# A two-layer graph convolution on one core: the short group of spans moved from the end of a layer to its start, and node numbers kept in PSUM

## The chip, the cores and the metric

The kernel runs on one core of a Trainium2 chip, in one launch. The metric is the device time of an execution in microseconds. A profile was taken of one execution; its span is the time from the first to the last instruction of the program. In the profile's rows PE is TensorE (matrix products), PEld its weight loads, DVE is VectorE, ACT is ScalarE, POOL is GpSimd, and SP is SyncE. PSUM is the memory that TensorE writes its products to; SBUF is the main on-chip memory.

## What is computed

`x` has 6250 nodes with 512 features; `src` and `dst` name 100,000 edges, sorted by `dst`. All in float32:

```python
h = relu(layernorm(x))
norm = -dinv[src] * dinv[dst]                 # dinv = 1/sqrt(number of edges out of a node), 0 where none
def cheb(h, W0, W1, b):
    tx1 = segment_sum(h[src] * norm[:, None], dst)   # a sum over the edges into each node
    return h @ W0 + tx1 @ W1 + b
g = cheb(h, W1_0, W1_1, b1)
g = leaky(layernorm(g) * gamma + beta, 0.01)
out = x + cheb(g, W2_0, W2_1, b2)
```

Each of the two layers therefore needs 100,000 rows of 2 KB fetched by index and summed by destination, and two 512 x 512 products for each node.

## The kernel before

**Units of the work.** The nodes are cut into 49 blocks of 128 rows (block 48 has 106). The edges are cut into 782 chunks of 128. A chunk is fetched by one indirect DMA on GpSimd's queue (L382, `gather_to`), which brings 128 rows of 512 numbers into one of 57 buffers of the tile `places` (`zr`, used in a ring). Rows come from a table in DRAM, `tab[0]` for layer 0 and `tab[1]` for layer 1, already scaled with `dinv`; only the first 60 chunks are fetched from `x` itself and brought to scale afterwards (`look_up`, `find`).

**Units, spans and groups.** A unit is a stretch of 3 chunks (`STEP`). It sums the edges into at most 32 (`Q`) consecutive nodes, starting with the node after the last one of the chunk ahead of it. It reads a span of 4 chunks, since its last node's edges may run on into the next unit's first chunk. There are 261 units (`NU`). Four units make a group (`NQ`), because four times 32 nodes fill the 128 partitions of a PSUM tile; that gives 66 groups (`NS`). In the kernel before, group g holds units 4g to 4g+3, and the last group, 65, is left with unit 260 alone.

**One group, `sums(g)` (L461).** VectorE adds 1 to 32 to the first node number of each unit (`node`, L465) and compares these with the destinations of the span's edges (`sel`, L474): a 0/1 matrix. `first`, `iota_r`, `node`, `dlx` and `sel` all lie in SBUF. TensorE multiplies `sel` with the gathered chunks (L480), 16 products for a whole group, each in two passes, each unit on a column tile of its own of 32 columns; the loop runs over the place in the span first and over the units second, so that consecutive products go to different column tiles. ScalarE copies the sums to SBUF (`agg`, L483).

**One block, `turn` and `dense`.** `turn(layer, i)` issues loads on SP's queue for a later block, transposes the block's own rows on TensorE (`own`, L451) and has ScalarE copy them (L453). Then `place` (L485) moves the sums of the groups that can hold nodes of this block to their rows: for every such group VectorE makes a 0/1 matrix `there` (L493) and TensorE runs four products (L496). `inside[i]` lists these groups; it is worked out from the mean number of nodes per group (`GN`, 96) with a slack of 32 nodes (`DRIFT`) to both sides, and `check` (L562) counts whether the edges really keep within it (if not, the slow `general_path` runs afterwards). VectorE scales the result (`aT`, L548). `dense` runs two sets of four products, for the own rows and for the sums (L458), and `finish` adds the bias (L511 in layer 0, L506 in layer 1), and normalises, activates and stores the rows for layer 1 (layer 0), or adds `x` and stores them to `out` (layer 1). Block 48's second bias is added to `x` beforehand (L542).

**What sets the order.** TensorE, GpSimd and SP run in the order of the program (`manual_schedule`, L372); the order on VectorE and ScalarE is made by the scheduler of the language. The loop is at L624: for each group it issues gathers up to 57 chunks ahead, runs `turn` for the blocks whose last group is behind, then `sums(g)`, then `dense` for these blocks. A gather waits until the last product that reads its buffer is done. After group 64 the loop finishes block 47, takes block 48's own rows through their products (`started`), and places groups 63 and 64 for it; after group 65 only that group's sums, its placing and block 48's last products are left. Layer 1 fetches rows that layer 0 stored, so its first gather waits for block 48's store of layer 0 (L527).

Of the kernel before, what the change touches and what calls it, by code (L numbers as in the profile page):

```python
# [19 lines left out]
P = 128  # L20
# [4 lines left out]
Q = 32  # L25
# [14 lines left out]
def gnn_kernel(  # L40
# [45 lines left out]
    NS = -(-NU // NQ)  # L86
    rows = [min(P, N - i * P) for i in range(NB)]
# [47 lines left out]

    edges = ctx.enter_context(ExitStack())
# [167 lines left out]
    with tc.tile_pool(name="turn", bufs=1) as wp, tc.tile_pool(  # L304
# [14 lines left out]
        first_ps = wps.tile([P, NQ * NS + 1], F32, name="first_ps")  # L319
# [3 lines left out]
        for k in range(2):  # L323
            for q in range(NQ):
                at = STEP * (q + k)
                nc.tensor.matmul(row_ps[q * Q : (q + 1) * Q, k, :], last.to_broadcast([P, Q]),
                                 dlx[:, at : at + STEP * NQ * (NS - 1) + 1 : STEP * NQ], start=True, stop=True)
# [27 lines left out]
def usual_path(tc, have):  # L355
    nc = tc.nc
    (x, out, tab, h_tab, ndinv_d, sidx, dlx, iota_r, w_sb, W2_1, W2_0, w_late, ident, eps, ones, first, node_of, minus,
     unsorted, ln, dinv, sdinv, bias1, bias2, gam, bet, unseen, N, E, D, NB, NC, NU, NS, KD, rows, places, order,
     groups, xs, sc, pick, src_lo, src_hi, p_id, dup) = (
        have[n] for n in ("x out tab h_tab ndinv_d sidx dlx iota_r w_sb W2_1 W2_0 w_late ident eps ones first node_of "  # L360
                          "minus unsorted ln dinv sdinv bias1 bias2 gam bet unseen N E D NB NC NU NS KD rows places "
# [4 lines left out]
    GN = NQ * STEP * P * N / E  # L366
    inside = [range(max(0, math.floor((i * P - DRIFT) / GN)), min(NS, math.ceil((i * P + r + DRIFT) / GN)))
              for i, r in enumerate(rows)]
    with ExitStack() as es:
# [91 lines left out]
        def sums(g):  # L461

            n = min(NQ, NU - NQ * g)
            node = pool.tile([P, NQ, Q], F32, name="node")
            nc.vector.tensor_tensor(node[:, :n, :], first[:, NQ * g : NQ * g + n, None].to_broadcast([P, n, Q]),  # L465
                                    iota_r[:, None, 1 : Q + 1].to_broadcast([P, n, Q]), op=OP.add)
            sel = pool.tile([P, NQ, SPAN, Q], F32, name="sel")
            chunk = [range(STEP * (NQ * g + q), min(STEP * (NQ * g + q) + SPAN, NC)) for q in range(n)]
            same = n if len(chunk[-1]) == SPAN else 1
            for q in range(0, n, same):  # L470
                w = len(chunk[q])
                of = dlx[:, 1 + chunk[q][0] : 2 + chunk[q][0]]
                of = bass.AP(tensor=of.tensor, offset=of.offset, ap=[of.ap[0], [STEP, same], [1, w], [0, Q]])
                nc.vector.tensor_tensor(sel[:, q : q + same, :w, :], of,  # L474
                                        node[:, q : q + same, None, :].to_broadcast([P, same, w, Q]), op=OP.is_equal)
            ps = psum.tile([P, D], F32, name="ps")
            for s in range(SPAN):
                for q in range(n):
                    if s < len(chunk[q]):
                        nc.tensor.matmul(ps[q * Q : (q + 1) * Q, :], sel[:, q, s, :], zr(chunk[q][s]), start=(s == 0),  # L480
                                         stop=(s == len(chunk[q]) - 1))
            agg[g] = pool.tile([P, D], F32, name="agg", bufs=4)
            nc.scalar.activation(agg[g][: n * Q], ps[: n * Q], AF.Copy)  # L483

        def place(i, some):  # L485
# [4 lines left out]
            for g in some:  # L490
                m = Q * min(NQ, NU - NQ * g)
                there = pool.tile([P, P], F32, name="there", bufs=3)
                nc.vector.tensor_scalar(there[:m, :r], iota_r[:m, :r], node_of[:m, g : g + 1], -(1.0 + i * P),  # L493
                                        op0=OP.subtract, op1=OP.is_equal)
                for kc in range(KD):
                    nc.tensor.matmul(placed[i][:, kc, :r], agg[g][:m, kc * P : (kc + 1) * P], there[:m, :r],  # L496
                                     start=(g == inside[i][0] and kc == 0),
                                     stop=(g == inside[i][-1] and kc == KD - 1))

        def finish(layer, i, v):  # L500
# [10 lines left out]
            nc.vector.tensor_add(v, v, bias1[:r])  # L511
# [50 lines left out]
        def check():  # L562
# [15 lines left out]
            for at, num, by, off in ((1, min(D, NC - 1), 1, 1), (1 + D, NC - 1 - D, 1, 1),  # L578
                                     (STEP, -(-(NC - SPAN) // STEP), STEP, 2)):
                if num > 0:  # L580
# [7 lines left out]
            nc.vector.scalar_tensor_tensor(of[:, :NS], iota_r[0:1, :NS], -GN, first[0:1, : NQ * NS : NQ], op0=OP.mult,  # L588
                                           op1=OP.add)
            nc.vector.tensor_mul(of[:, :NS], of[:, :NS], of[:, :NS])  # L590
            count(of[:, :NS], OP.is_gt, float(DRIFT * DRIFT))
# [26 lines left out]
        for layer in range(2):  # L618
# [5 lines left out]
            for g in range(NS):  # L624
# [3 lines left out]
                else:  # L628
                    gather_to(layer, STEP * NQ * g + R)
# [3 lines left out]
                if layer == 0:  # L633
                    look_up("hT_ps")
                    find("hT_ps")
                    assert looked >= min(RAW, STEP * NQ * (g + 1) + 1)
# [4 lines left out]
                sums(g)  # L641
# [14 lines left out]
                if g == NS - 2:  # L656
                    while inside[i].stop < NS:
# [5 lines left out]
                    products(started[i], last_hT[layer], w_late[:, 1] if layer else w_sb[1], rows[i], True)  # L663
                    place(i, inside[i][:-1])
# [323 lines left out]
```

## Time and profile before

| | |
|---|---|
| median of 3 runs | 2149.52 us (2146.58 to 2150.33) |
| the profiled execution | 2148.89 us |
| its span | 2146.7 us |
| granted TensorE clock, mean | 0.926 of full |
| POOL busy | 1520.2 us (71%) |
| gathers from the tables (L382, x1504) | 1444.5 us, 960 ns each |
| products of the sums (L480, x4168 passes) | 732.4 us busy, 280.7 us idle ahead of them |
| placing (L496, x2080 passes) | 253.8 us busy |
| DMA over the span | 527.05 MB, mean 246 GB/s |
| gathers of layer 0, first from the table and last (start) | 172.6 us, 1087.69 us |
| gathers of layer 1, first and last (start) | 1123.74 us, 2109.66 us |

The page's group lines read: line of the kernel, engine, operation, tile written, tiles read, count | busy time, mean ns of one | idle time of the engine ahead of them, and what ended it. "issue" means that the engine waited for nothing that the profile shows. In the timeline a line is: start in us, duration in us, engine, line, operation, tiles, shapes, count, and in brackets the idle time ahead with what ended it. A float32 product shows as two passes. GpSimd's spans are those of the instruction[...], not of the transfer; a transfer lands some us after its instruction began (median 4.0 us).

### The profile page before, as it was taken

How to read it: one execution, taken by the hardware profiler on the slowest of the kernel's cores; microseconds unless marked ns; L12 is line 12 of the kernel's file. 1: busy time of each engine (PE TensorE's matmuls, PEld its weight loads, DVE VectorE, ACT ScalarE, POOL GpSimd, SP SyncE). 2: the span in 40 equal slices, each digit the busy share in tenths (PEclk: the TensorE clock that was granted, in tenths of full speed). 3: DMA queues.
4: the chain of work that ended last, by engine and by line, in shares of the span. 5: the costliest groups of instructions: out<-in, count | busy, mean ns of one | idle time of the engine just before them, and what ended most of it. 6: DMA issues, size and time to landing. Idle time of an engine off the chain costs nothing.

```text
span 2146.7 us, 23527 instructions
## 1 busy us (share of the span) xinstructions
PE 1795.7 (84%) x8843; PEld 794.7 (37%) x8843; DVE 674.8 (31%) x1341; ACT 382.7 (18%) x694; POOL 1520.2 (71%) x1577
## 2 busy tenths in 40 slices
PE   5669888988879888988876888889888888889888
PEld 4534333333334333433331333334333333334333
DVE  8974323333334233333330212212212212211211
ACT  7774212111112122111110000000000000000000
POOL 5067777777777777777727777777777777777772
PEclk9779999999989999999997989999999999999989
DMA  9298888788788888788837788888878888877883
GB/s 368 82 354 264 247 254 254 242 250 255 243 286 249 253 255 250 240 255 244 254 121 229 243 251 256 255 251 245 256 243 255 243 251 257 256 248 247 245 252 117
DMA packets 198945, 527.05 MB, mean 246 GB/s; under 512 B 31864, under 2 KB 46019, under 8 KB 198822
## 3 DMA queue, kind: packets, MB, share of 16 engines
q0 software_dynamic: 125120, 410.09, 62.4%
q1 hardware_dynamic: 73702, 115.36, 15.5%
q8 instruction: 71, 1.16, 0.2%
q14 instruction: 52, 0.43, 0.1%
HBM read 474.06 MB, written 51.27 MB: 245 GB/s over the span
## 4 chain that ended last, share of the span: by engine, by line
PE 48%; DMA 29%; POOL 9%; issue 8%; DVE 5%; ACT 0%; POOLq 0%; SPq 0%; ACTq 0%; DVEq 0%
DMA places<-tab,sidx 28%; PE u_ps L458 25%; PE ps L480 15%; POOL places L382 9%; PE aT_ps L496 5%; PE hT_ps L451 1%; DVE hi L252 1%; DVE lo L252 1%; DVE places L393 0%; PE both_ps L258 0%; DMA places<-in_x_dram,sidx 0%; DVE places L394 0%; PE u_ps L422 0%; PE hT_ps L422 0%; DVE both L428 0%
## 5 line engine op out<-in xcount | busy, mean ns | idle before, releaser
L382 POOL DMA_INDIRECT places<-tab,sidx x1504 | 1444.5, 960 | 493.8 <-issue 315.8
L480 PE MATMUL ps<-places,sel 128*32 128x512 f32 x4168 | 732.4, 666 | 280.7 <-DMA places<-tab,sidx 268.1
L480 PEld LDWEIGHTS ps<-places,sel 128*32 128x32 f32 x4168 | 141.8, 117 | 781.0 <-DMA places<-tab,sidx 591.3
L474 DVE TENSOR_TENSOR sel<-dlx,node 128x512 f32<-128x512 f32 x132 | 90.9, 688 | 750.0 <-PE ps L480 750.0
L496 PE MATMUL aT_ps<-there,agg 128*128 128x128 f32 (+2 forms) x2080 | 253.8, 278 | 1.4 <-ACT agg L483 1.4
L496 PEld LDWEIGHTS aT_ps<-there,agg 128*128 128x128 f32 (+1 forms) x2080 | 246.1, 196 | 4.2 <-ACT agg L483 3.2
L483 ACT ACTIVATE agg<-ps 128x512 f32<-128x512 f32 x132 | 78.8, 597 | 918.9 <-PE ps L480 918.9
L458 PE MATMUL u_ps<-places,hT 128*128 128x512 f32 (+1 forms) x392 | 185.8, 618 | 0.7 <-ACT hT L453 0.7
L458 PE MATMUL u_ps<-w,hT 128*128 128x512 f32 (+1 forms) x392 | 181.1, 605 | 0.7 <-ACT hT L453 0.7
L458 PE MATMUL u_ps<-places,aT 128*128 128x512 f32 (+1 forms) x392 | 178.0, 597 | 0.7 <-DVE aT L548 0.7
L458 PE MATMUL u_ps<-w,aT 128*128 128x512 f32 (+1 forms) x392 | 176.3, 592 | 0.7 <-DVE aT L548 0.7
L506 DVE TENSOR_TENSOR u_ps<-u_ps,bias 128x512 f32<-128x512 f32 x48 | 33.6, 700 | 294.9 <-PE u_ps L458 294.9
L511 DVE TENSOR_TENSOR u_ps<-u_ps,bias 128x512 f32<-128x512 f32 (+1 forms) x49 | 34.3, 700 | 284.3 <-PE u_ps L458 284.3
L453 ACT ACTIVATE hT<-hT_ps 128x512 f32<-128x512 f32 (+1 forms) x98 | 58.3, 595 | 349.6 <-PE hT_ps L451 348.2
L458 PEld LDWEIGHTS u_ps<-places,hT 128*128 128x128 f32 (+1 forms) x392 | 72.3, 195 | 117.3 <-issue 116.5
L458 PEld LDWEIGHTS u_ps<-w,hT 128*128 128x128 f32 (+1 forms) x392 | 70.3, 189 | 109.0 <-issue 106.5
L458 PEld LDWEIGHTS u_ps<-places,aT 128*128 128x128 f32 (+1 forms) x392 | 74.8, 191 | 95.4 <-issue 94.6
L458 PEld LDWEIGHTS u_ps<-w,aT 128*128 128x128 f32 (+1 forms) x392 | 74.3, 190 | 94.3 <-issue 93.4
L382 POOL DMA_INDIRECT places<-in_x_dram,sidx x44 | 45.0, 1024 | 86.8 <-ACT places L396 57.7
L448 ACT ACTIVATE h<-h,ln 128x512 f32<-128x512 f32 (+1 forms) x49 | 39.7, 813 | 283.3 <-DMA h<-in_x_dram 283.3
L493 DVE TENSOR_SCALAR there<-iota_r,node_of 128x128 f32<-128x128 f32 x260 | 76.6, 295 | 38.7 <-PE aT_ps L496 38.6
L548 DVE TENSOR_TENSOR aT<-aT_ps,to 128x512 f32<-128x512 f32 (+1 forms) x98 | 67.1, 685 | 39.4 <-PE aT_ps L496 37.9
(128 smaller groups left out, 942.7 us busy)
## 6 DMA issues: line engine op xcount, KB each, us to landing
places<-tab,sidx POOLq DMA_INDIRECT x1504
h<-in_x_dram SPq DMA_DIRECT2D x48, 256.0 KB
tab<-t SPq DMA_DIRECT2D x48, 256.0 KB
h_tab<-g SPq DMA_DIRECT2D x48, 256.0 KB
h<-h_tab SPq DMA_DIRECT2D x48, 256.0 KB
xt<-in_x_dram SPq DMA_DIRECT2D x48, 256.0 KB
out_dram<-t SPq DMA_DIRECT2D x48, 256.0 KB
places<-in_x_dram SPq DMA_DIRECT2D x4, 1792.0 KB
```

What stands on the lines that cost most here:

```text
L252: nc.vector.tensor_tensor(t, s[:, g * 2 * GJ : (g + 1) * 2 * GJ].rearrange("p (j s) -> p j s", s=2)[:, :, None, :] .to_broadcast([EP, GJ, ...
L382: nc.gpsimd.indirect_dma_start(out=zr(t), out_offset=None, in_=x if layer == 0 and t < RAW else tab[layer], in_offset=bass.IndirectOffsetO ...
L448: nc.scalar.activation(h[:r], h[:r], AF.Relu, bias=ln[:r, 1, i : i + 1], scale=ln[:r, 0, i : i + 1])
L453: nc.scalar.activation(hT[:, :, :r], ps[:, :, :r], AF.Copy)
L458: nc.tensor.matmul(u_ps[:r], hT[:, kc, :r], w[:, kc, :], start=(start and kc == 0), stop=(not start and kc == KD - 1))
L474: nc.vector.tensor_tensor(sel[:, q : q + same, :w, :], of, node[:, q : q + same, None, :].to_broadcast([P, same, w, Q]), op=OP.is_equal)
L480: nc.tensor.matmul(ps[q * Q : (q + 1) * Q, :], sel[:, q, s, :], zr(chunk[q][s]), start=(s == 0), stop=(s == len(chunk[q]) - 1))
L483: nc.scalar.activation(agg[g][: n * Q], ps[: n * Q], AF.Copy)
L493: nc.vector.tensor_scalar(there[:m, :r], iota_r[:m, :r], node_of[:m, g : g + 1], -(1.0 + i * P), op0=OP.subtract, op1=OP.is_equal)
L496: nc.tensor.matmul(placed[i][:, kc, :r], agg[g][:m, kc * P : (kc + 1) * P], there[:m, :r], start=(g == inside[i][0] and kc == 0), stop=(g ...
L511: nc.vector.tensor_add(v, v, bias1[:r])
L548: nc.vector.tensor_tensor(aT[:, :, :r], placed.pop(i)[:, :, :r], to.pop(i)[:, None, :r].to_broadcast([P, KD, r]), op=OP.mult)
```

## The change

The short group moves from the end to the start of a layer: `unit[g]` is the first unit of group g, group 0 holds unit 0 alone, and groups 1 to 65 hold four units each. Every use of the fixed stride is rewritten with it: the gathers' reach, `inside`, `place`, `row_ps` (which numbers the nodes for `there`, now in two products for each where there was one) and `check`. The bound between groups 64 and 65 gets its own, smaller slack, so that group 65 counts for block 48 alone; block 47's last group is then 64.

The first node numbers stay in PSUM, in a tile `nodes_ps` of one whole bank that lives as long as the kernel; `node` is a corner of the same tile. So L465 and L474 read one operand from PSUM and one from SBUF. `first` in SBUF stays for `check`.

`sums` is split: `choose` makes `node` and `sel`, `sums` the products. For the last group, `choose` runs ahead of block 47's work, and its products are put in the order of their chunks, not of their place in the span. Block 48's bias of layer 0 is added by a product of a row of ones with one row of `bias1` on top of its own products; the addition at L511 is left out for it.

```diff
+    unit = [max(0, NU - NQ * (NS - g)) for g in range(NS + 1)]
...
+    nodes_ps = stay.enter_context(tc.tile_pool(name="nodes_ps", bufs=1, space=bass.MemoryType.PSUM)).tile(
+        [P, D], F32, name="nodes_ps")
...
-        first_ps = wps.tile([P, NQ * NS + 1], F32, name="first_ps")
+        first_ps = nodes_ps[:, : NQ * NS + 1]
...
             for q in range(NQ):
-                at = STEP * (q + k)
-                nc.tensor.matmul(row_ps[q * Q : (q + 1) * Q, k, :], last.to_broadcast([P, Q]),
-                                 dlx[:, at : at + STEP * NQ * (NS - 1) + 1 : STEP * NQ], start=True, stop=True)
+                for g, n in ((0, 1), (1, NS - 1)):
+                    at = STEP * (unit[g] + q + k)
+                    nc.tensor.matmul(row_ps[q * Q : (q + 1) * Q, k, g : g + n], last.to_broadcast([P, Q]),
+                                     dlx[:, at : at + STEP * NQ * (n - 1) + 1 : STEP * NQ], start=True, stop=True)
...
-    GN = NQ * STEP * P * N / E
-    inside = [range(max(0, math.floor((i * P - DRIFT) / GN)), min(NS, math.ceil((i * P + r + DRIFT) / GN)))
-              for i, r in enumerate(rows)]
+    UN = STEP * P * N / E
+    mean = [UN * u for u in unit[:NS]] + [N]
+    drift = [0] + [DRIFT] * (NS - 2) + [min(DRIFT, int(mean[NS - 1]) - (NB - 1) * P), 0]
...
+        some = [g for g in range(NS) if mean[g] - drift[g] < i * P + r and mean[g + 1] + drift[g + 1] > i * P]
+        inside.append(range(some[0], some[-1] + 1))
...
-        def sums(g):
-            n = min(NQ, NU - NQ * g)
-            node = pool.tile([P, NQ, Q], F32, name="node")
-            nc.vector.tensor_tensor(node[:, :n, :], first[:, NQ * g : NQ * g + n, None].to_broadcast([P, n, Q]),
+        def choose(g):
+            at, n = unit[g], unit[g + 1] - unit[g]
+            node = nodes_ps[:, D - P :].rearrange("p (q e) -> p q e", q=NQ)
+            nc.vector.tensor_tensor(node[:, :n, :], nodes_ps[:, at : at + n, None].to_broadcast([P, n, Q]),
                                     iota_r[:, None, 1 : Q + 1].to_broadcast([P, n, Q]), op=OP.add)
             sel = pool.tile([P, NQ, SPAN, Q], F32, name="sel")
...
+                    nc.vector.tensor_tensor(sel[:, q : q + k, :w, :], of,
+                                            node[:, q : q + k, None, :].to_broadcast([P, k, w, Q]), op=OP.is_equal)
+            return sel, chunk
+        def sums(g, sel, chunk):
...
-            for s in range(SPAN):
-                for q in range(n):
-                    if s < len(chunk[q]):
-                        nc.tensor.matmul(ps[q * Q : (q + 1) * Q, :], sel[:, q, s, :], zr(chunk[q][s]), start=(s == 0),
-                                         stop=(s == len(chunk[q]) - 1))
+            todo = [(s, q) for s in range(SPAN) for q in range(n) if s < len(chunk[q])]
+            if g == NS - 1:
+                todo.sort(key=lambda t: chunk[t[1]][t[0]])
+            for s, q in todo:
+                nc.tensor.matmul(ps[q * Q : (q + 1) * Q, :], sel[:, q, s, :], zr(chunk[q][s]), start=(s == 0),
+                                 stop=(s == len(chunk[q]) - 1))
...
-            nc.vector.tensor_add(v, v, bias1[:r])
+            if i < NB - 1:
+                nc.vector.tensor_add(v, v, bias1[:r])
...
-                    gather_to(layer, STEP * NQ * g + R)
+                    gather_to(layer, STEP * unit[g] + R)
...
-                sums(g)
+                sums(g, *(chosen if g == NS - 1 else choose(g)))
...
                 if g == NS - 2:
+                    chosen = choose(NS - 1)
                     while inside[i].stop < NS:
                         dense(layer, i, *turn(layer, i))
...
                     products(started[i], last_hT[layer], w_late[:, 1] if layer else w_sb[1], rows[i], True)
+                    if layer == 0:
+                        nc.tensor.matmul(started[i][: rows[i]], ones[0:1, : rows[i]], bias1[0:1, :], start=False,
+                                         stop=False)
                     place(i, inside[i][:-1])
```

## The prediction

> **What bounds the kernel now.** I read the page first, then GpSimd's waits, then the gathers' own line, then single gathers in the timeline, and last TensorE's timeline at the end of a layer.
>
> ```profile
> PE 1795.7 (84%) x8843; PEld 794.7 (37%) x8843; DVE 674.8 (31%) x1341; ACT 382.7 (18%) x694; POOL 1520.2 (71%) x1577
> PE 48%; DMA 29%; POOL 9%; issue 8%; DVE 5%; ACT 0%; POOLq 0%; SPq 0%; ACTq 0%; DVEq 0%
> L382 POOL DMA_INDIRECT places<-tab,sidx x1504 | 1444.5, 960 | 493.8 <-issue 315.8 <-DMA places<-tab,sidx 90.9 <-DMA tab<-t 35.1
> ```
>
> The busy shares and the chain point to TensorE. The group line says otherwise: 1,504 gathers on GpSimd, 960 ns each, with 493.8 us of idle time "before" them. The question is whether that idle time is waiting. GpSimd's waits, us in total, times, longest:
>
> ```profile
> POOL places L382 <- issue: 320.7, 1052, 0.3
> POOL places L382 <- DMA places<-tab,sidx: 90.9, 298, 0.3
> POOL places L382 <- PE ps L480: 30.3, 98, 0.8
> ```
>
> 1,448 waits, and but for a single one they are the same 0.30 us, whatever is named. So it is the price of issuing a gather, and GpSimd issues back to back. From the 61st gather on, an undisturbed start-to-start step is 1.253 us (mean of the 1,433 steps under 1.29 us). Layer 1 has its first gather at 1123.74 and its last at 2109.66: 985.9 us for 781 steps, of which 781 x 1.253 = 978.6 is the bare rhythm. Layer 0 from gather 61 on: 915.1 us for 721 steps, 903.5 bare. Nothing but the rate of GpSimd sets these 1,901 us; TensorE only follows. What is above the bare rhythm is 11.6 us in layer 0 and 7.3 in layer 1, in 69 long steps. One of them, GpSimd and VectorE in the timeline:
>
> ```profile
> 1191.45 0.95 POOL L382 DMA_INDIRECT places<-tab,sidx  x1 [0.30 <-issue]
> 1192.65 0.69 DVE L474 TENSOR_TENSOR sel<-dlx,node 128x512 f32<-128x512 f32 x1 [8.59 <-PE ps L480]
> 1192.70 1.46 POOL L382 DMA_INDIRECT places<-tab,sidx  x1 [0.30 <-DMA places<-tab,sidx]
> 1194.47 0.94 POOL L382 DMA_INDIRECT places<-tab,sidx  x1 [0.30 <-DMA places<-tab,sidx]
> ```
>
> The comparison `sel` began 0.05 us ahead of the gather and ended at 1193.34; the gather took 1.46 instead of 0.95. I sorted all gathers by the VectorE instruction that was running 0.125 us after the gather began. `sel` (L474): 70 gathers, 61 of them stretched, 17.7 us in all. `node` (L465): 10, 6 stretched, 0.4. `there` (L493): 20, 5 stretched, 0.2. Instructions with one operand in PSUM and one in SBUF (L506, L507, L511, L519, L521, L525, L530, L548): 179 gathers, none stretched.
>
> The rest of the span is the two turns of a layer, in which GpSimd stands: 36.05 us from the last gather of layer 0 (1087.69) to the first of layer 1, and 37.0 from the last gather (2109.66) to the end. TensorE at the first:
>
> ```profile
> 1086.39 1.07 PE L480 MATMUL ps<-places,sel 128*32 128x512 f32 x8 [1.19 <-DMA places<-tab,sidx]
> 1087.65 1.06 PE L480 MATMUL ps<-places,sel 128*32 128x512 f32 x8 [0.19 <-DMA places<-tab,sidx]
> 1089.01 2.14 PE L480 MATMUL ps<-places,sel 128*32 128x512 f32 x10 [0.29 <-DMA places<-tab,sidx]
> 1091.08 0.66 PE L451 MATMUL hT_ps<-ident,h 128*128 128x128 f32 x4
> 1091.57 2.84 PE L496 MATMUL aT_ps<-there,agg 128*128 128x128 f32 x24
> 1094.25 3.60 PE L458 MATMUL u_ps<-w,hT 128*128 128x512 f32 x8
> 1097.69 3.60 PE L458 MATMUL u_ps<-w,aT 128*128 128x512 f32 x8
> 1101.12 0.53 PE L451 MATMUL hT_ps<-ident,h 106*128 106x106 f32 x4
> 1102.32 3.68 PE L458 MATMUL u_ps<-w,hT 128*106 128x512 f32 x8 [0.68 <-ACT hT L453]
> 1105.84 1.93 PE L496 MATMUL aT_ps<-there,agg 128*128 128x106 f32 x16
> 1107.70 1.90 PE L480 MATMUL ps<-places,sel 128*32 128x512 f32 x4
> ```
>
> Group 64 waits for chunk 780, the last but one; from there TensorE has a full queue to the last span.
>
> **Node numbers in PSUM.** `sel` and `node` each lose one SBUF input. Removed: 18.9 us of long steps, less one wait of 0.5 us on TensorE and 0.5 to 0.9 for `there` and an `is_hi`, which stay: 17.7. All of it lies on the path, since GpSimd never waits in these stretches; 0.3 more comes from gathers 32 to 60. The Trainium skill, "SBUF — State Buffer", Who interferes with whom, gives the reason: a VectorE instruction with two SBUF inputs takes a port that GpSimd needs to read SBUF, and whichever comes second waits for the whole of the first. By that rule a gather would start within a `sel` 0.693/1.253 = 55% of the time and wait 0.35 on average: 132 x 0.19 = 25 us. The rows say 17.7, since `sel` must still run 0.125 us into the gather; the rows count. Cost: `sel` 0.693 becomes about 0.70, as the additions on PSUM (L506, L511: 0.700); 134 x 0.01 us on an engine 31% busy, and `sel` is made a group ahead. Bounds: nothing gained if one SBUF input is enough to hold GpSimd, 18.5 at most. I take 18.0, because of the 179 to 0.
>
> **Setup.** `row_ps` (L326) goes from 8 products to 16, half of them one column wide; its passes now come every 0.12 us on each column tile. It delays `node_of`, and behind it the loads and the table store, by 0.1 to 0.3: take 0.2. Group 0 with one unit makes less work, early, where nothing waits for it.
>
> **More groups per block.** With boundaries shifted by 24 nodes nearly every block meets 3 groups: 290 `there` for 260, and 120 more products at L496, 240 passes x 0.11 = 27 us of TensorE. It lies in TensorE's waits for gathers (L480: 268 us). If that cover went, all 27 would count.
>
> **The last group.** Units 257 to 260 form the last group, only block 48 needs it, and block 47 needs 63 and 64. Group 64 now ends with chunk 771, ten gathers earlier; block 46's products fall behind group 64, where they were ahead of it. I write the queue from the last gather's start, G. Chunk 771 was issued at 1075.16 and landed at 1079.90 (G-7.8); in layer 1 at G-8.4. Group 64 ends 1.0 later (1090.10 to 1091.08): G-6.8 and G-7.4. Then block 46's products 7.07 (2101.88 to 2108.95), block 47's transposes and 16 placing passes 2.3 (a group fewer than the 3.2 above), its products 6.87, block 48's transposes 1.2, own products 3.5, in layer 0 the bias product 0.87 (two passes of 0.43), 8 placing passes 0.93, and the last sums. These were 2 products; they are 14, 3.7 us if they run like a full group (2098.31 to 2102.05). Sum 26.5 and 25.6: the copy of the sums starts at G+19.7 and G+18.2; it started at G+21.95 (1109.64) and G+21.92. Gains 2.2 and 3.7. In layer 0 the bias addition (L511, 0.70, plus 0.03) goes from the end: 0.7. Together 6.7. That the queue is full also means that sorting by chunk buys nothing: all chunks have landed by then.
>
> The sort may cost. In chunk order two or three products in a row go to one column tile. The Trainium skill, "TensorE: Matmul & The Clock Gate", Part 3, says matmuls start and end strictly in order. Then 19 rounds of 0.43 run where 8 do: +4.7 per layer, and both gains are gone. The trace speaks against it: L282's products go twice to the lower, then twice to the upper column tile, and their first two passes start at 87.519 and 87.532, which for one tile would be 0.1 apart. Reordering over two products is shown, over seven not. With four passes queued per tile I get +1.7; between 0 and 4.7 I take 0.8 per layer, nearer to the end the trace shows. Other uncertainty: TensorE could still be 3 us behind in layer 1, where the clock fell to 0.83 in the last stretches; and block 48's last products, 5.38 us at 2134.04 against 3.68 at 1112.11, may run 1.7 faster. Tails: 6.7 - 1.6 = 5.1, from -5.7 to 8.4. DVE stays ahead: `sel` of the last group is made before block 47, and layer 1's `sel` stands behind the last sums but ends before `aT` needs VectorE (0.98 us against 1.8).
>
> **Sum.** The profiled execution: 2148.89, of which the span is 2146.7 and 2.2 lies around it. Span 2146.7 - 18.0 - 5.1 + 0.2 = 2123.8; with 2.2: 2126.0. The median of the runs shown is 0.6 above the profiled one: 2126.6, say 2127.
>
> **Rivals.**
> *The sort eats the tails* (0.20): TensorE keeps order; 4.7 per layer lost, gain of the ports alone: 2149.5 - 18 + 3 = 2134.
> *The port is held all the same* (0.07): one SBUF input suffices; tails alone: 2144.4. Against it: 179 to 0.
> *TensorE becomes the bound* (0.05), slower: the 27 us of placing passes stretch the run if TensorE falls so far behind that a gather finds its buffer unread. With 57 buffers and 12 to a group that is some 40 gathers, 50 us. Three blocks in four groups are 4 x 3.6 + 3 x 7.7 + 9 x 0.93 = 45.9 us per 60.2 us of gathers; the clock would have to be granted under 0.76 throughout (0.95 and 0.93 in the two layers). Time: 2149.5 + 27 - 5 = 2171.
> *Gains and costs cancel* (0.06): GpSimd finds another limit near the old rate, about 2148; no row shows one.
> My case keeps 0.62.
>
> Under 0.2% (4.3 us) a measurement of this kernel can't be told from no change, so the line is at 2145.2 and 2153.8. Faster: 0.62 + 0.20 and most of the held port, 0.88; same 0.07; slower 0.05. Range: best ports and best tails give 2123, less the runs' own scatter 2120; worst tails with the ports' gain 2138.
>
> **What would show it.** Right: the gathers' mean falls from 960 to about 949 ns, no step over 1.29 with `sel` beside it, last-to-last gather about 979 us in layer 1; the pause at the turn about 33 us for 36.05. Wrong: long steps that stay (port), the 28 last passes at L480 spread over 8 us (sort), waits of GpSimd on TensorE over 0.8 us (bound).

## The result and the profile after

| | before | after |
|---|---|---|
| median of the runs on the same chip | 2148.05 us (2144.5 to 2150.33, 4 runs) | 2123.31 us (2119.62 to 2124.38, 4 runs) |
| profiled execution / its span | 2148.89 / 2146.7 us | 2123.42 / 2121.6 us |
| layer 0, from the 61st gather to the last | 915.1 us | 901.6 us |
| turn: last gather of layer 0 to first of layer 1 | 36.05 us | 34.85 us |
| layer 1, first gather to last | 985.9 us | 976.6 us |
| end: last gather to the end | 37.05 us | 36.89 us |

The ratio is 0.9887, with a 95% interval of 0.987 to 0.9904. The changed kernel is 1.1% faster; 2127 was forecast. Of the 25.1 us between the two spans, 22.8 lie in the two stretches of gathers, 1.4 in the turn and the end, and 0.9 ahead of the 61st gather. The kernel before takes 2148 to 2151 us beside the runs up to e8, but 2554 and 2529 us on the two chips of e9 to e12, so no absolute time of those four is used.

The page of the changed kernel, the lines that answer to the three shown of before, and TensorE's sums:

```profile
PE 1802.3 (85%) x9101; PEld 822.6 (39%) x9101; DVE 684.9 (32%) x1375; ACT 383.2 (18%) x694; POOL 1497.5 (71%) x1577
PE 49%; DMA 27%; POOL 10%; issue 9%; DVE 4%; ACT 0%; POOLq 0%; SPq 0%; ACTq 0%
L392 POOL DMA_INDIRECT places<-tab,sidx x1504 | 1422.5, 946 | 491.8 <-issue 314.1
L499 PE MATMUL ps<-places,sel 128*32 128x512 f32 x4168 | 714.4, 665 | 243.6 <-DMA places<-tab,sidx 234.3
```

The same 1,504 gathers take 946 ns each for 960; their idle time has hardly moved (491.8 for 493.8). TensorE has 258 more instructions and 7 us more of work, and waits for gathers 234 us. GpSimd's waits, us in total, times, longest:

```profile
POOL places L392 <- issue: 318.6, 1045, 0.6
POOL places L392 <- DMA places<-tab,sidx: 98.1, 322, 0.3
POOL places L392 <- PE ps L499: 23.8, 78, 0.3
```

The longest wait on TensorE is 0.3 us, which is the price of issuing a gather. So GpSimd still never waits for a buffer, although TensorE has more to do. One gather that begins under a `sel` in the changed kernel:

```profile
450.42 0.69 DVE L487 TENSOR_TENSOR sel<-dlx,nodes_ps 128x512 f32<-128x512 f32 x1 [0.48 <-PE ps L499]
450.51 0.95 POOL L392 DMA_INDIRECT places<-tab,sidx  x1 [0.30 <-DMA places<-tab,sidx]
...
451.76 0.94 POOL L392 DMA_INDIRECT places<-tab,sidx  x1 [0.30 <-issue]
```

This is the place in the rhythm at which the gather of before took 1.46 us: `sel` begins 0.09 us ahead and lasts 0.6 us into it. Now the gather takes 0.95 and the next one comes 1.25 us later. Sorted in the same way as before (counted are the comparisons that began ahead of the gather and were still running 0.125 us after its start), 63 gathers have a `sel` beside them, and none is stretched; of 44 with a `there` beside them 12 are, by 0.5 us in all.

TensorE at the end of layer 0; the last gather, G, begins at 1073.31:

```profile
1062.74 3.64 PE L499 MATMUL ps<-places,sel 128*32 128x512 f32 x32
...
1083.58 3.68 PE L468 MATMUL u_ps<-w,hT 128*106 128x512 f32 x8 [0.68 <-ACT hT L463]
1087.19 1.10 PE L689 MATMUL u_ps<-bias,ones 1*106 1x512 f32 x2
1088.23 1.14 PE L515 MATMUL aT_ps<-there,agg 128*128 128x106 f32 x8
1089.30 5.40 PE L499 MATMUL ps<-places,sel 128*32 128x512 f32 x28
1095.42 1.14 PE L515 MATMUL aT_ps<-there,agg 128*128 128x106 f32 x8 [0.73 <-ACT agg L502]
1097.26 3.68 PE L468 MATMUL u_ps<-w,aT 128*106 128x512 f32 x8 [0.69 <-DVE aT L568]
```

Group 64's sums take 3.64 us without a wait and end at G-6.9; the forecast was G-6.8, but behind a wait for chunk 771. The other thing that differs is the last line but two: the 28 sorted passes of the last group take 5.40 us, where 32 unsorted ones take 3.64.

### The profile page after: what moved, and what is told of

It reads as the page before. It is cut to its first block, busy times and chain, and to the rows that moved or that the text cites. A ratio compares the mean times of both kernels' runs of the same rounds, so it can differ in the third digit from the quotient of the medians.

```text
span 2121.6 us, 24132 instructions
## 1 busy us (share of the span) xinstructions
PE 1802.3 (85%) x9101; PEld 822.6 (39%) x9101; DVE 684.9 (32%) x1375; ACT 383.2 (18%) x694; POOL 1497.5 (71%) x1577
## 4 chain that ended last, share of the span: by engine, by line
PE 49%; DMA 27%; POOL 10%; issue 9%; DVE 4%; ACT 0%; POOLq 0%; SPq 0%; ACTq 0%
DMA places<-tab,sidx 27%; PE u_ps L468 24%; PE ps L499 16%; POOL places L392 10%; PE aT_ps L515 7%; PE hT_ps L461 1%; DVE hi L256 1%; DVE lo L256 1%; PE both_ps L262 1%; DMA places<-in_x_dram,sidx 0%; DVE places L403 0%; PE hT_ps L432 0%; DVE places L404 0%; PE u_ps L432 0%; DVE xt L420 0%
## 5 line engine op out<-in xcount | busy, mean ns | idle before, releaser
L392 POOL DMA_INDIRECT places<-tab,sidx x1504 | 1422.5, 946 | 491.8 <-issue 314.1
L499 PE MATMUL ps<-places,sel 128*32 128x512 f32 x4168 | 714.4, 665 | 243.6 <-DMA places<-tab,sidx 234.3
L487 DVE TENSOR_TENSOR sel<-dlx,nodes_ps 128x512 f32<-128x512 f32 (+3 forms) x134 | 89.9, 672 | 693.8 <-PE ps L499 693.8
L515 PE MATMUL aT_ps<-there,agg 128*128 128x128 f32 (+2 forms) x2320 | 279.8, 277 | 4.8 <-ACT agg L502 4.8
L515 PEld LDWEIGHTS aT_ps<-there,agg 128*128 128x128 f32 (+1 forms) x2320 | 270.7, 194 | 8.7 <-ACT agg L502 6.8
L502 ACT ACTIVATE agg<-ps 128x512 f32<-128x512 f32 (+1 forms) x132 | 78.7, 596 | 886.0 <-PE ps L499 885.9
L525 DVE TENSOR_TENSOR u_ps<-u_ps,bias 128x512 f32<-128x512 f32 x48 | 33.6, 699 | 297.7 <-PE u_ps L468 297.7
L531 DVE TENSOR_TENSOR u_ps<-u_ps,bias 128x512 f32<-128x512 f32 x48 | 33.6, 700 | 289.5 <-PE u_ps L468 289.5
L512 DVE TENSOR_SCALAR there<-iota_r,node_of 128x128 f32<-128x128 f32 (+1 forms) x290 | 85.7, 296 | 42.1 <-PE aT_ps L515 40.4
```

The costliest lines, as they stand in the source:

```text
L392: nc.gpsimd.indirect_dma_start(out=zr(t), out_offset=None, in_=x if layer == 0 and t < RAW else tab[layer], in_offset=bass.IndirectOffsetO ...
L487: nc.vector.tensor_tensor(sel[:, q : q + k, :w, :], of, node[:, q : q + k, None, :].to_broadcast([P, k, w, Q]), op=OP.is_equal)
L525: nc.vector.tensor_add(v, v, bias2[:r])
```

## The experiments

The theory from the profile: GpSimd's rate sets both layers; a VectorE comparison with two SBUF inputs holds the gather that starts under it; TensorE's full queue sets the turn and the end. The rivals: the gain is the regrouping's, or the gathers' rate is a matter of the chip or the execution. There are twelve runs: e1 to e4 on one chip, e5 to e8 on another, e9 and e10 on a third, e11 and e12 on a fourth.

For comparison, the same stretches in the profiles of the two kernels and of e1 to e8 (us; the first column is when the 61st gather starts; "undisturbed" is the mean of the steps under 1.29 us, "excess" what is above it in both layers):

| | 61st gather | layer 0 | turn | layer 1 | end | undisturbed | excess |
|---|---|---|---|---|---|---|---|
| before, first profile | 172.6 | 915.1 | 36.05 | 985.9 | 37.05 | 1.2531 | 18.9 |
| before, second (e5) | 175.3 | 911.5 | 36.16 | 984.7 | 37.06 | 1.2503 | 18.2 |
| after | 171.7 | 901.6 | 34.85 | 976.6 | 36.89 | 1.2502 | 0.4 |
| e1, node numbers in PSUM alone | 172.3 | 901.8 | 37.99 | 976.3 | 37.07 | 1.2502 | 0.4 |
| e2, regrouping alone | 174.2 | 907.6 | 34.88 | 985.3 | 33.88 | 1.2509 | 14.1 |
| e3, after without the sort | 174.4 | 901.8 | 33.97 | 977.1 | 32.83 | 1.2507 | 0.4 |
| e4, block 48's own part early | 174.4 | 901.5 | 26.44 | 976.3 | 27.78 | 1.2501 | 0.1 |
| e6, more comparisons, two in SBUF | 173.3 | 913.3 | 34.27 | 976.5 | 34.16 | 1.2502 | 12.0 |
| e7, more comparisons, one in PSUM | 174.4 | 902.3 | 34.96 | 977.2 | 34.31 | 1.2510 | 0.5 |
| e8, own parts of 47 and 48 early | 176.2 | 902.4 | 25.89 | 977.1 | 25.49 | 1.2510 | 0.5 |

**e1, the node numbers alone.** To the kernel before:

```diff
-        first_ps = wps.tile([P, NQ * NS + 1], F32, name="first_ps")
+        first_ps = nodes_ps[:, : NQ * NS + 1]
...
-            node = pool.tile([P, NQ, Q], F32, name="node")
-            nc.vector.tensor_tensor(node[:, :n, :], first[:, NQ * g : NQ * g + n, None].to_broadcast([P, n, Q]),
+            node = nodes_ps[:, D - P :].rearrange("p (q e) -> p q e", q=NQ)
+            nc.vector.tensor_tensor(node[:, :n, :], nodes_ps[:, NQ * g : NQ * g + n, None].to_broadcast([P, n, Q]),
```

> The kernel before with one part of the change: the first node numbers and `node` lie in PSUM, the groups stay as they were. My theory: the long gather steps beside `sel` (17.7 us in the profile of before) go, the tails stay, so some 18 us less than before (2130), up to 22 if the 3 ns by which the undisturbed step fell in the changed kernel (1.2502 for 1.2531 us, 3.9 us over 1,502 steps) belong to this part too. Rival A, the gain comes from the other grouping (fewer or differently placed comparisons): about 0. Rival B, the 3 ns are a matter of the chip or the run: the step stays at 1.253 here and the gain is 18.

Measured: 2128.41 us (before 2147.57), ratio 0.991, 95% interval 0.9895 to 0.9925, that is 19.2 us faster. Excess 0.4 us for 18.2. The theory holds, and rival A falls: this half of the change brings three quarters of the gain without any new grouping. Its turn is 1.8 to 1.9 us longer than before; block 48's last products took 5.38 us there for 3.68, of which more below.

**e2, the regrouping alone.** To the changed kernel:

```diff
-            node = nodes_ps[:, D - P :].rearrange("p (q e) -> p q e", q=NQ)
-            nc.vector.tensor_tensor(node[:, :n, :], nodes_ps[:, at : at + n, None].to_broadcast([P, n, Q]),
+            node = pool.tile([P, NQ, Q], F32, name="node")
+            nc.vector.tensor_tensor(node[:, :n, :], first[:, at : at + n, None].to_broadcast([P, n, Q]),
```

> The changed kernel with `node` written into SBUF again, from the first node numbers in SBUF, so that `sel` and `node` have two SBUF inputs; the new grouping, the sort and the bias product stay. My theory: the long steps come back (about 18 us in 60 to 70 gathers beside `sel`), and only the tails' 1.4 us are left of the gain: about 2146, some 20 us slower than the changed kernel. Rival A, the gain is the grouping's: about 2123, no long steps. Rival B, the 3 ns of the undisturbed step go with the operands: then 1.253 here, and 2147 to 2149.

Measured: 2138.96 us, ratio 0.9958 (0.9945 to 0.9972), 8.6 us faster than before where 1.4 was expected. The direction is the theory's: 51 of 58 gathers beside `sel` are stretched again, 12.8 us, and the kernel is 15 us behind the changed one. The size is a miss, for two reasons in the table. The excess is 14.1 us and not 18: fewer gathers start under a `sel` with the new groups, 58 for 70 (layer 0: 5.7 us for 10.0, layer 1: 8.4 for 8.2). That the new groups moved `sel` to another place in the gathers' rhythm is a reading, not tested. And the end is 3.2 us shorter than before, where the changed kernel's own profile shows 0.2. So the two halves don't simply add: alone they bring 19.2 and 8.6 us, 27.8 together, and both at once 24.7.

**e5, the kernel before once more.** No edit.

> The kernel before, unchanged, profiled once more. In the profile shown first the undisturbed step from gather to gather is 1.2531 us; in the changed kernel and in four variants of it or of the kernel before it is 1.2501 to 1.2509. Reading A, the 3 ns belong to that first profiled execution (its chip or its hour): 1.250 here, with long steps of 17 to 19 us in all, and a span some 4 us under 2146.7. Reading B, they belong to the kernel: 1.253 again.

Measured: 2148.06 us against 2150.54 of the runs beside it, ratio 0.9992 (0.9976 to 1.0009).

```profile
L382 POOL DMA_INDIRECT places<-tab,sidx x1504 | 1440.5, 958 | 493.1 <-issue 315.3
```

958 ns for 960, and the undisturbed step is 1.2503: reading A. 4.3 of the 22.8 us (2.9 ns on each of 1,502 steps) by which the gathers' stretches differ between the first two profiles belong to the first execution, not to the change. Against this second profile the layers are 9.9 and 8.1 us shorter, 18.0 together. Reading A also asked for a span 4 us shorter; it is 2.0 (2144.7), because the 61st gather started 2.7 us later. That start lies between 171.7 and 176.2 in the ten profiles, with no order by kernel.

**e6 and e7, a second comparison behind each `sel`.** To the changed kernel; nothing reads `more`. The first three lines are e6's; e7 differs in the last line alone, which takes `node` in PSUM for `iota_r` in SBUF:

```diff
+                    more = pool.tile([P, NQ, SPAN, Q], F32, name="more", bufs=1)
+                    nc.vector.tensor_tensor(more[:, q : q + k, :w, :], of,
+                                            iota_r[:, None, None, 1 : Q + 1].to_broadcast([P, k, w, Q]), op=OP.is_equal)
...
+                                            node[:, q : q + k, None, :].to_broadcast([P, k, w, Q]), op=OP.is_equal)
```

> The changed kernel with a second comparison of `sel`'s size behind each `sel`, its result never read, with both inputs in SBUF (the node numbers `dlx` and the constants `iota_r`): 130 more VectorE instructions of about 0.69 us. My theory (a comparison with two SBUF inputs holds the gather that starts under it until it ends): 60 to 70 gathers are stretched, 14 to 19 us in all, so about 2139. Rival, the long steps came from elsewhere (TensorE's reads, the place of `sel` in the queue): no long steps, 2123.

> The same second comparison, with its node numbers taken from `node` in PSUM, one input in SBUF. My theory: no gather is stretched and the 90 us more of VectorE cost nothing, 2123 within 2. Rival, VectorE's load or its writes into SBUF count, whatever the inputs: as much as with two inputs in SBUF, about 2139, or in proportion to the writes, some 5 us or more.

Measured: e6 2137.44 us, ratio 0.9944 (0.9926 to 0.9962); e7 2124.31 us, ratio 0.987 (0.9854 to 0.9886). The two differ by 13.1 us, and their programs only in where the second operand lies. In e6 `more` waits for no product, so the scheduler ran all 134 of them ahead of 350 us instead of one per group. That makes the test sharper: of the 132 steps from the 61st gather to 350 us 56 are long, with 11.6 us of excess; of the 1,370 later ones 5, with 0.3 us. 57 of the 59 gathers that have a `more` beside them are stretched, none of the 59 beside a `sel` in the same kernel. In e7, 52 gathers have a `more` beside them, and none is stretched. A row of eight `more` in e6:

```profile
281.53 5.76 DVE L490 TENSOR_TENSOR more<-dlx,iota_r 128x512 f32<-128x512 f32 x8
282.30 1.46 POOL L392 DMA_INDIRECT places<-tab,sidx  x1 [0.30 <-issue]
...
284.06 1.15 POOL L392 DMA_INDIRECT places<-tab,sidx  x1 [0.30 <-issue]
285.51 1.15 POOL L392 DMA_INDIRECT places<-tab,sidx  x1 [0.30 <-DMA places<-tab,sidx]
```

VectorE is busy for 5.76 us without a pause, and still each gather loses only 0.2 to 0.5 us. It waits for the comparison under which it began, not for the row of them.

**e3, no sort.** To the changed kernel:

```diff
-            if g == NS - 1:
-                todo.sort(key=lambda t: chunk[t[1]][t[0]])
```

> The changed kernel without the sort by chunk of the last group's products; they run in the usual order, turn by turn over the four column tiles. In the changed kernel the 28 passes took 5.40 us in both layers; a full group of 32 takes 4.2, so 28 should take 3.7. My theory (TensorE holds only a few passes per column tile, so runs of two or three products on one tile leave the others idle): 1.7 us less per layer, 3.4 in all, about 2120. Rival, the 5.40 is the price of the last group itself and not of the order: 0. A third case, the order lets the sums start before the last chunk has landed and so is worth something: slower than the changed kernel by up to 1 us.

Measured: 2121.64 us, ratio 0.9874 (0.9859 to 0.9889); the interval overlaps that of the changed kernel. 3.4 was not seen in the time. In the profiles turn and end together are 4.9 us shorter than in the changed kernel's, but the 61st gather starts 2.7 us later and the layers take 0.7 longer. The end of layer 0:

```profile
1091.39 3.63 PE L497 MATMUL ps<-places,sel 128*32 128x512 f32 x28
1095.78 1.14 PE L513 MATMUL aT_ps<-there,agg 128*128 128x106 f32 x8 [0.76 <-ACT agg L500]
1097.61 5.38 PE L468 MATMUL u_ps<-w,aT 128*106 128x512 f32 x8 [0.69 <-DVE aT L566]
```

The same 28 passes take 3.63 us, 1.77 less, in both layers: the first theory, as far as TensorE goes. The order cost this in every profile that has the sort (5.40, eight ends in four profiles), and in none without. But block 48's last products took 5.38 instead of 3.68 in layer 0: their passes come up to 0.86 us apart and then 0.43 again, and the profile's granted clock in that stretch is 0.55. So the turn was 0.9 us shorter and not 1.8. The end was 4.1 us shorter; what is beyond the sort there is taken up in the section on the prediction.

**e4, block 48's own part ahead.** To e3's kernel: its rows are loaded at group 57, and multiplied at group 61 (the expectation names both one too low):

```diff
+                if g == NS - 5:
+                    started[NB - 1] = psum.tile([P, D], F32, name="hT_ps")
+                    last_hT[layer] = own(layer, NB - 1)
+                    products(started[NB - 1], last_hT[layer], w_late[:, 1] if layer else w_sb[1], rows[NB - 1], True)
+                    if layer == 0:
+                        nc.tensor.matmul(started[NB - 1][: rows[NB - 1]], ones[0:1, : rows[NB - 1]], bias1[0:1, :],
+                                         start=False, stop=False)
...
-                    last_hT[layer] = own(layer, i)
-                    started[i] = psum.tile([P, D], F32, name="u_ps")
-                    products(started[i], last_hT[layer], w_late[:, 1] if layer else w_sb[1], rows[i], True)
```

> The changed kernel without the sort, and with block 48's own part (its rows' load, two transposes, 8 passes, in layer 0 the bias product) moved ahead to the stretch where TensorE still waits for gathers: loaded at group 56, computed at group 60, kept in one buffer of PSUM. My theory (at the end of a layer TensorE has a full queue, so every us taken out of that queue comes off the time): 1.2 + 3.5 per layer, and 1.1 for the bias product in layer 0, that is 10.5 us, with the sort's 3.4 some 14 us: about 2109. Rival: block 48's own part fills waits that otherwise stand open at the end (for the last chunk, for the copies on ScalarE and VectorE), so only half of it or less comes off: 2114 to 2120.

Measured: 2109.44 us (2108.21 to 2110.66), ratio 0.9823 (0.9809 to 0.9836). That is 2109 as the theory said, 13.9 us under the changed kernel's median and 12.2 under e3's. Turn and end are 8.4 and 9.1 us shorter than in the changed kernel's profile. The work was not reduced, only moved: in layer 1 the own products now run at 2028.4, 50 us or 40 gathers ahead of the last gather.

```profile
1063.39 4.80 PE L498 MATMUL ps<-places,sel 128*32 128x512 f32 x32
...
1080.76 3.60 PE L469 MATMUL u_ps<-w,aT 128*128 128x512 f32 x8
1084.19 1.04 PE L514 MATMUL aT_ps<-there,agg 128*128 128x106 f32 x8
1085.16 3.63 PE L498 MATMUL ps<-places,sel 128*32 128x512 f32 x28
```

Block 48's transposes and own products no longer stand between block 47's products and the placing. Group 64's sums take 4.80 us, 1.2 over the bare 3.64: they wait for their last chunk, so TensorE is not behind there. They end at 1068.2, 7.7 us ahead of the last gather (1075.89).

**e8, block 47's own part as well.** To e4's kernel: block 47's rows are loaded early too (the products run at groups 60 and 62, where the expectation names 61 for block 47), and the last sums run in two halves around block 47's products:

```diff
+                if g in (NS - 6, NS - 4):
+                    k, name = (NB - 1, "hT_ps") if g == NS - 6 else (NB - 2, "u_ps")
+                    started[k] = psum.tile([P, D], F32, name=name)
+                    products(started[k], own(layer, k), w_late[:, 1] if layer else w_sb[1], rows[k], True)
...
+                    ps = sums(NS - 1, *chosen, None, range(SPAN // 2))
+                    dense(layer, i, hT, aT)
+                    sums(NS - 1, *chosen, ps, range(SPAN // 2, SPAN))
```

> The version with block 48's own part ahead of the end, and beyond it: block 47's own part ahead as well (rows loaded at group 59, 2 x 4 passes at group 61), and the last group's sums in two halves, one ahead of block 47's products and one behind. My theory (TensorE's queue at the end of a layer is full, each us taken out of it comes off): 4.2 us per layer less than that version, as block 47's transposes and own products (0.6 + 3.6) leave the queue, about 2101. Rival: the queue is now so short that the last chunk's landing (3.7 us after its issue, and 2 more) and block 47's chain on VectorE end last: half of it or less, 2105 to 2109.

Measured: 2104.49 us (2103.26 to 2108.81), ratio 0.9785 (0.9771 to 0.9798), the fastest kernel here. It gains 5.0 us on e4 by the medians, where 8.4 was expected; the two ran on different chips, and by the ratios it would be 8. The profile is of the slowest of its five runs and shows 2.8 us less at the turn and the end together:

```profile
1071.07 3.64 PE L499 MATMUL ps<-places,sel 128*32 128x512 f32 x32
...
1085.35 3.70 PE L469 MATMUL u_ps<-w,aT 128*128 128x512 f32 x8
1088.98 1.92 PE L499 MATMUL ps<-places,sel 128*32 128x512 f32 x12
1090.82 2.03 PE L517 MATMUL aT_ps<-there,agg 128*128 128x106 f32 x16
```

Group 64's sums now take the bare 3.64 us, with no wait in them, and end 3.9 us ahead of the last gather (1078.56) instead of 7.7. TensorE has no slack left there, so the work that was moved from the end to group 62 pushed everything behind it: in layer 0, 3.8 us of the 4.2 that left the end came back in front of it. The turn is 0.5 us shorter than e4's, the end 2.3.

**e9 and e11, the own parts at groups 42 and 48.** To e8's kernel, as in e8 but with

```diff
-                if g in (NS - 6, NS - 4):
+                if g in (NS - 24, NS - 18):
```

> The version with the own parts of blocks 47 and 48 ahead, but moved much further: block 48's at group 42, block 47's at group 48, in place of 60 and 62. There the version before left TensorE with a full queue from 30 us before the last gather on, so the moved 9 us came out of the end only to lie in front of it: group 64 began 7.5 us before the last gather, where with block 48 alone moved it began 12.5 before it. My theory: at groups 42 and 48 TensorE still has waits for gathers enough to take them up, group 64 begins some 12 us before the last gather again, and both ends become 4 to 5 us shorter: about 2096. Rival: the end is by now set by the landing of the last chunks and by the chain over VectorE, or TensorE is behind already at group 48: 2104 as with the nearer place.

> The kernel of e9 once more, since in its call every kernel, the one before included, took 18% longer (before: 2554 us). Where the kernel before takes its usual 2148 to 2151, the expectations are those of e9. My theory: group 64 begins some 12 us before the last gather, both ends become 4 to 5 us shorter than with the nearer place, about 2096. Rival, other limits hold the end (landing, VectorE, a TensorE that is behind already at group 48): 2104.

Measured: 2518.52 us against 2554.03 of before (ratio 0.986, 0.9837 to 0.9883), and 2506.39 against 2528.71 (0.9913, 0.989 to 0.9935). Whether the further place brings the 2096 is not answered.

**e10 and e12, the changed kernel once more.** No edit.

> The changed kernel once more. Its first profile has 36.9 us from the last gather to the end; four profiles with the same products at the end have 33.9 to 34.3 (with the sort) and 32.8 (without). My reading: in the first profile TensorE's granted clock was 0.83 in the 10 us that lie 20 to 10 us before the last gather, behind its last wait for a gather, 1.00 in the others, and TensorE brought that delay to the end. With a clock of 1.00 there this profile shows 34 to 34.5; with 0.83 again, 36 to 37. Rival, the 36.9 are the changed kernel's own and the variants' instructions shift it: 36.9 whatever the clock.

> The changed kernel once more, as in e10, for the same reason. My reading: with a granted clock of 1.00 in the stretch 20 to 10 us before the last gather of layer 1, 34 to 34.5 us from that gather to the end; with 0.83 as in its first profile, 36 to 37. Rival, the 36.9 are the changed kernel's own: 36.9 whatever the clock.

Measured: 2540.78 us against 2554.03 (ratio 0.9951, 0.9933 to 0.9969), and 2528.51 against 2528.71 (0.9999, 0.9984 to 1.0014): on these chips the change brings half a per cent and nothing. In their profiles TensorE has hundreds of waits that nothing explains (of e12: `PE aT_ps L515 <- issue: 195.5, 202, 16.4`), and GpSimd no longer issues back to back: in e12 gathers wait for TensorE up to 10.4 us. What the gain above rests on, GpSimd's own rate, does not set the time there. Why these chips took longer was not found, and the question of e10 and e12 is answered below only from the other profiles.

## Why the prediction was right, point by point

**GpSimd sets both layers.** Shown. e7 added 90 us of VectorE work, the change itself 258 instructions on TensorE, and e4 and e8 moved TensorE's work into the stretch of the gathers; in all of them the layers stayed at 901.5 to 902.4 and 976.3 to 977.2 us. It does not hold on the chips of e9 to e12.

**The ports, -18.0.** Shown, in kind and in size: 18.0 against the second profile of before, 19.2 in e1 by the medians. The first pair of profiles gives 22.8, but 4.3 of that is the rhythm of one execution. The evidence that was chosen, 179 gathers beside one operand in PSUM and none stretched, was the right one; e6 and e7 repeat it with a single operand moved. The rule that the prediction cites from the Trainium skill ("SBUF — State Buffer", Who interferes with whom), that a VectorE instruction with two SBUF inputs contends with GpSimd's reads of SBUF, fits these comparisons: 61 of 70 gathers stretched with two, none of 63 with one. Its bare form gave 25 us; the rows' 17.7 was the better number. `sel` was expected to become 0.01 us longer and became as much shorter (687 ns for 696, whole groups alone).

**Setup, +0.2.** Not resolved: the start moves by 4.5 us between profiles.

**More groups, at nothing.** Held in the layers. 290 `there` and 2,320 passes at L515 ran, and TensorE's waits for gathers shrank from 268 to 234 us. The longest wait of GpSimd on TensorE is 0.3 us. At the end of a layer, where TensorE has no wait left to fill, they are not free: the placing ahead of group 64 takes 2.84 us for three groups, where two take 1.95.

**The tails, -5.1.** The forecast was too high, for two reasons. The first is the sort. 0.8 us a layer was taken for it, nearer to the end at which TensorE reorders freely; it costs 1.77, which is the forecast's own middle case of four passes queued per column tile (+1.7). Strict order, as the Trainium skill has it ("TensorE: Matmul & The Clock Gate", Part 3), would have cost 4.7 by the forecast's estimate.

The second is the wait ahead of the queue. Group 64 was to wait for chunk 771 and so to end at G-6.8 and G-7.4. It waited in neither layer: TensorE came to it late, out of a queue that was full already. In layer 0 this ends at nearly the same moment, G-6.9, and the rest of the sum fits: the last sums end at G+21.4, which is 19.6 without the sort's 1.77, and 19.7 was forecast. That the start agrees is luck. In layer 1 the same group ends at G-3.8, 3.6 us late, though chunk 771 had landed at G-8.6 (2072.22 + 3.9). Layer 1 of the changed kernel, and of e7, which has the same products there:

```profile
2064.49 1.26 PE L499 MATMUL ps<-places,sel 128*32 128x512 f32 x2 [1.98 <-DMA places<-tab,sidx]
2065.69 5.13 PE L468 MATMUL u_ps<-places,hT 128*128 128x512 f32 x8
...
2077.30 3.64 PE L499 MATMUL ps<-places,sel 128*32 128x512 f32 x32
```

```profile
2067.88 1.05 PE L502 MATMUL ps<-places,sel 128*32 128x512 f32 x2 [1.50 <-DMA places<-tab,sidx]
2068.86 3.70 PE L468 MATMUL u_ps<-places,hT 128*128 128x512 f32 x8
...
2079.04 3.64 PE L502 MATMUL ps<-places,sel 128*32 128x512 f32 x32
```

With the last gathers at 2084.73 and 2088.84, group 64 ends at G-3.8 and G-6.2. Of these 2.4 us, 1.6 are the clock: behind the wait of 1.98 us the next passes run in part at half rate (5.13 us for 3.70, 1.26 for 1.05; granted clock 0.83 from G-20 to G-10, for 1.00 in e7). The other 0.7 is the wait itself, which ends that much later before G. e2 and e6 are like e7 (G-6.7 and G-6.2). Their ends, 33.9 to 34.3 us, are 2.7 to 3.2 shorter than before. That TensorE "could still be 3 us behind in layer 1" was named as an uncertainty.

The 37.05 us of before is not firm either. In its first profile block 48's last products take 5.38 us there; in the second they take 3.68, and the last sums end 1.9 us later after G. The two ends come out equal (37.05 and 37.06) by chance.

**The sum.** The two profiled executions, term by term (us gained):

| | forecast | measured |
|---|---|---|
| ports (excess 18.9 to 0.4) | 18.0 | 18.5 |
| undisturbed step (1.2531 to 1.2502) | 0 | 4.3 |
| turn and end | 5.1 | 1.4 |
| ahead of the 61st gather | -0.2 | 0.9 |
| span | 22.9 | 25.1 |

The ports, three quarters of the gain, were forecast from the right cause. That the sum came so near is in part luck: the tails fell 3.7 us short, and the step's 4.3, which nobody forecast and e5 shows not to be the change's, made up for it. By the medians the gain is 24.7 us; its parts can't be told apart there.

**The marks that the prediction set.** No step over 1.29 us with `sel` beside it, and waits on TensorE of 0.3 us: as forecast. 946 ns for 949, and 976.6 us for 979 in layer 1: the difference is the step's. The turn took 34.85 us for about 33 (33.9 by the forecast's own terms, its 0.8 for the sort included), and the 28 passes 5.40 us: both are the sort, though not the 8 us that were set as its sign of being wrong.

**The rivals.** The port is not held by one SBUF input (e1, e7). TensorE does not become the bound: GpSimd's waits for TensorE stay at 0.3 us. The sort ate 3.5 of the 6.7 us of the tails, not 9.4.

**What was missed.** The larger gain at the end lay in the full queue that the prediction itself wrote out, line by line. Block 48's own products stood in it and needed nothing that was late; moved ahead, they bring 12 us (e4), more than twice the regrouping's tails.

## What to carry to other kernels

Where one engine issues back to back and sets the rate, sort its long steps by what else ran just then; if they all lie beside one kind of instruction, moving a single operand of that instruction can remove them, and an instruction of the same kind with its result unread shows on the chip whether that is the cause. A queue that is full at the end of a stage gets shorter by moving out work whose inputs are early, but only to where the queue still has waits: at group 61 one block's part still found room, and a second one at group 62 came back at the end. Products that share the array by column tiles should go round the tiles; grouping them by tile cost half as much again.

## What the runs showed of the hardware

- A gather is stretched by more than 0.1 us only if a comparison with two SBUF inputs began ahead of it and still runs about 0.125 us after the gather's start, and then until that comparison ends (in the 62 stretched ones of before to 0.012 us). Of the 15 comparisons in before that began within 0.125 us after a gather's start none stretched it; the next one in a row of them does not hold it (e6: 0.2 to 0.5 us each). Per comparison this is 0.14 us in the kernel before (17.7 us in 125) and 0.10 in e2 and e6.
- TensorE overtakes among column tiles, but only so far. In the sorted group six passes in a row go to the first tile, 0.43 us each; the second tile's first pass starts 0.89 us after the first one's, ahead of three passes that were issued before it, and the third and fourth follow 0.89 us apart. (The trace does not name the tile; which pass belongs to which is read from the 0.43 us between starts.)
- The granted clock falls to half for 3.4 us behind short waits: at the end of a layer two of 0.7 us, for ScalarE's and VectorE's copies, were enough at four ends (the first profile of before in layer 1, e1 in both layers, e3 in layer 0), and not at the others. Each time the eight passes that follow take 5.38 us for 3.68. In every profile the changes of the clock lie whole multiples of 3.41 us apart. At the four ends both waits fall between two neighbouring points of this grid; at the twelve ends where a grid point lies between or inside the two waits the clock stayed at full. At two (e2 and e7 in layer 1) both fall together and it stayed at full too, which is not explained.
- The undisturbed step of the gathers is 1.2501 to 1.2531 us from one execution to another, which over 1,502 steps is up to 4.5 us of a kernel's time.
